# First loads in larger pieces, x by halves of the batch, and a new order of the first and last steps of a conditional GRU

## The chip, the cores and the metric

One core of one Trainium2 chip runs the whole program. The metric is the device time of one execution in microseconds; the kernel before takes 1233.74 us in the median of three runs. Readings of its trace are of one profiled execution.

## The reference, cut to what matters

Batch 64, 128 steps, input and hidden width 512, all fp32:

```
def step(h, inp):
    x_t, prop = inp
    comb = concatenate([x_t, h])
    z = sigmoid(comb @ Wz + bz)
    r = sigmoid(comb @ Wr + br)
    h_cand = tanh(concatenate([x_t, r * h]) @ Wh + bh)
    h_new = (1 - z) * h + z * h_cand
    h_next = where(prop, tanh(h_new @ Wp + bp), h_new)   # prop: every 4th step but the last
    return h_next, h_new
out = x + all h_new
```

Each W of a gate is 1024 x 512: its upper 512 rows meet x_t, the lower 512 meet h. The first h is an input (called cond in the profile, h0 in the code).

## The kernel before, in words

**Layout.** The batch is split into two halves of 32 (h = 0, 1), a width of 512 into four quarters q. A tile such as `xj`, x of one step, has on its 128 partitions the 32 samples of each of the four quarters, and the two halves side by side. VectorE turns it by 32x32 blocks into `xT`, the stationary operand of TensorE. `wx` holds the upper rows of the three gates, as pieces (gate, k) with k = 0 to 3 of 128 rows each; `wh` the lower rows; `wp` Wp.

**The x part** does not depend on the recurrence. For steps 0 to 3 it is plain: 48 units of 16 matmuls, one for each (step, gate, k), into the banks a, x, q, y, b and z (function `plain`); VectorE adds the bias and stores the result in `cp`. From step 4 on, four steps are a group, and their products follow a scheme of seven products in place of eight, on two levels. Its operands are sums: of weights (`tw`, `tf`, `tt`; made once, by `weigh` on GpSimd, called POOL, and VectorE, called DVE) and of xT (`s12r`, `s`, `o` and others, POOL). A batch's results leave the banks q, a, y and x by copies on ScalarE (called ACT) and additions on DVE, are put together in `st` by POOL, and reach `cp` by a DMA for one half and a copy on ScalarE for the other (`place`).

**The h part** of a step: the products hT with wh for r (bank e for half 0, bank r for half 1), sigmoid on ScalarE, r*h and its transpose `rhT` on DVE, the products rhT with Wh, tanh, and the update of h, its transpose `hT`. From the third step to the fifth last the products with r and z share seven products (`sa`, made by POOL from hT).

**Start.** TensorE first runs 42 idle matmuls on zeros. Three one-row loads bring br, bz and bh; `spread` multiplies them with a row of ones, so that all partitions hold them; it is one operation of 12 groups of matmuls, four for each bias, and the units of the x part stand behind it on TensorE. ScalarE copies its result out.

**Order.** A planner holds each operation with its engine, what it reads and what it writes. The order of all operations is the table ORDER, a compressed list of positions; each engine executes its own in that order. Loads are issued by an engine's queue: SP, ScalarE (`actq`) or POOL (`poolq`). The transfers of SP and ScalarE share eight counters, dealt out in turn; POOL's have eight of their own. A transfer waits, at the head of its engine, until the one that used its counter eight transfers ago has landed (`[waits DMAHW5_49]` in an order). So a load on ScalarE can hold ScalarE's later work.

Lines below ORDER move up by some 43 in the changed kernel: the helper of all products is line 412 before and 406 after, the spreading 925 and 882, the transposes of x 566 and 523, the sums of weights 611 and 568, the bias loads 493 and 473, the copy to cp 884 and 841.

Of the kernel before, what the change touches and what calls it, by code (L numbers as in the profile page):

```python
# [172 lines left out]
1ET<%P9Y}BV#L@GFvmexgoPDBU|Fy%+F2SnGsiIu&H!pR%g)ijNG2FC~M6u%V1$?Mq)f}$nehM3|^91lxYPvW$3pTW$^sW;tcxE+|1tWcjsm1W$H7%neUL
<8B~|i>NDH2c;=v-pP2)*8JSs`_qE#0yVEn%0J8w|p?_^gW@=`T%CyWB5U3_2PaeEIwV7%Fnv|)@pvf7zDubj68Gb@WoR}G(k;i4k8JW*X)tQNaaha;j<P
0yMayWyP!DWrjlx4iqj7UdiMrDNZOl5|U(o9K)6=q0zrYJ*7GKCqf2<}P&2$Y{u$v{$+!H<(qqyFS!f*vIOiE=Nwmmv90BHT`p!rw^lCU=q>3D1jAgij8`
H<G@Dzm{A}ZYNigQ2eh;NpB)vOlD>-CYKYR?@NXVD927G*>g$uB+O1GXA=8FayrR7nb^mmv!jX4eiQ9W*#0EFCt-V%aCfpl*_DL5lI|o9yONzrS{K5tNw_
7^ydfKtZOO)DOJXs{-I{Dj_~iQ=6WiXJY)#VNi<c*MM-r`0P<zsrEKg`#(w?+FK?i)>9m!fC`~b8k%`k6++MXb_5&Ee_ZAcmuW^s!W*;tTJyfB%U@M?X+y
-n&8naoVSAR#<0nV#UO$(&?rGBdfDysp$FQxa)vGCBFY^hR~US0xjZ*AFF?2@)nH<C95Xg$kHfCNEEd(wsqKlb6ONV-kK|raYMdE9FT=^5R4&FO@=E3cfT
Mo6r-`)KST(M5VL@T1g@gPlhKlElNfwMTt_FKs-DtNa)7osgeY2aWc490O1Iz193r;52^$%w;0^0gglNPLHH;hmJEZ6@{|6U?M(2)nBI@?$GAVf7vsC}ot
WH?@pODM4sOKU^%#?@@vZn~d^P6q?f6;@!`zJ+--)jSs$gx%h4@ljm)wf8*f<xTi!a2eC+>~U0`v=U`gE-KLV7AT&cr8U{REUV@rf7($6_=ZABj~D9gPpg  # L180
2V-;~9*&)T@xIvI8#~VK_&~fn4gz#A_IAhKz8G6wgIl(_FOE0G|7MySWAq2KCf3))>*CdbwNI+v8ME#2gLr+sDn@JLHStOaSH}Kt*FwD#tIOlcL~W04p8H
ixEaLW<VYMNqzg!$6nOhJqj%7427RCA)33ub!u`JJu5s#+FGveuB`R_3_4b+s_u8F6{bVD*3bWJ=tUY}UgVuU8f9I1}+gcwbUC&Azw6>(Lpjf>wK7mtl6#
$Wq7nh=-874cU~AuoljG)B^>Cw){bjf|xu@rYO|iATrM@OXHPiU&(kEEU3ckstF#@i4gf&lSWau~ZiGLQy=BE`&1%(kMUnAEgJ<tRI5@bbp$TfL%f!r`hB
5y>x!ey5qZPax+bDrHOVUeLZ~>s9j5Qs4q?M<@BenrZ1)O#q`BALejbP`LxuN=Fg@TemFjr7S5(mruoy5*2R5kUdYF1(<jn04_oL+`Wf+P`cQh1htupJ44
88ueI(8HrR^cd(+AS_f%N_~v${dD?dh&`dPkZ?+tTLdbo3h|4A-UCrCAWHPH#xB1|*$nv^q`GE7H8n+SAUmw6`+dmj21|bZgpif7F`x+S8t!w5FTV9qF9g
o^DAmN-s$_r=7)VYjK(`OzTbQMwn8vBt0*!pG>0@>4j+*&rUma=~?MHK&L)EGtD?uo32eGGAlhbJuS^@(lu#>tJ4&rs<cv-u1q80tuyJ0H0IHm^w{*I^qB
O7G<$ta8jVYr0+z+)X*L?ftE18_F)dGzOqZw2()<Wm-jIH?G(9T)>hSdF^oTTHJh)SoeidXv`juh`hYkZjEL{N12NtIJ-RXgdK8^~~P##6B|9^_|AX=YR*
yHG4#2!X>BkBHNO8cXS5q<gr?A(v~qubGwbM8gtW<<&L=tgusVz;6z5!VN&+=%+3YY`!rBh(x9g1H{8OkauyaWTRdA;RY)4);V{Pejf{^mIgfqEpe?=xOJ
CRD%gV8=Z*GMCg2kj8jo{8b0}*i;hPJqTHG2V00wX_ec99v=8*&2px*lgHgOILg}5666}b&Bh}v)1>MosNbxpD@H@U3Z-_QW+oBDCBJ9$&5$BN3Xia3{m6
3}&BFk=%IwNaYq_jnPd(<A8D<VVhh?YlxXo*%uO;KC4EV>gdjas2E1&_48s1eW-HGpr3{HAD0<TpHViz8p71ka1+MPxzb|7swb6D^1^R~O;BNdGyW9?gu5  # L190
8xf*YBQ!PQ(Bw$0jxZLhqA5{T#0z**#6B7qRYnyN8yhk95vCTRqayrmczcyZ#nHF0S`ZaPSStd93I~tj(O17VJ>8!gNEJk18AwTm(SuYzP<oKMpVIpwy_f
1w-Ag?H-UmKRp{>zfi0*<B??6#+r`AOB?UW+lNTKVgJE_~L>nU_E#XnBnfGy#TTd8X)bR%^$brlAz59aI&IPr1{e!umlZl(GF2%S%H=Tlcw=TmU|ICLg;G
KEg16!<`ulF$o>Q-@MWeQJM7-j|Zmfz;mAo|LNWO7Y#PBD^!jKffcTrnjYdWlL&DYJ2Lx%cJg;xIeWuCFY*mmJ&CnkgzGWJ~hY<Fkhb<vNgs2xIVQeg=n%
aMdP(8+L2nF>PW3hErY&1McbjYgQ0DyxD9k`s^tmdrKzQ<SZjilf+ZkT)|gt9a^kQF+W%^Vy=NLzO8|3I^HcPv3sX*GN}iKioSL2D=BDbPN!-j7$>?MntV
~T!2kwDd3w>G&O;1fprMJResez15PNC|Q_<>F<Qxj9-gcRn4iqyCi&yPvbcgs^{DT7i}p5jKqox*RU5h<}C^~HizeoD+wEs2!32SR0S>T|OrB%u2t|2RZ<
!~T$m@n;9ZTOmVtLV7)<FWn5UhBw0NP+z83!keI9x*T2$?}UT(a@YsF0=ycsRjFQx=%uhXq!*#c7Y2{>q0*3|(xvchNY967LfR8v44=LTCxRUu)6?O(koA
VAASdKRcrxUU4<4srb~ro={%CkSBuAhf1{@0sT97&j{a|<?qz6L0FAVpGcuz=}*Bz1}T_LT;+e4>2+!<~QG2RuTZQ-DSzw~y8UE#*CIEA*uD6=ut*F&%++
#YTMudfZ)hG<>5Ce+aCa9!9Lrqq=oS{1GgSAansVMjO$JMCdR_`ym`u-zKAh7MU8TJ2$TXj!dcOK3HO8vbt=HHDTvFVxM&;i3@Lhla5v{NvnkVOST=3VTA
N&j2+eoCy~<Bh+Vyv@To#H((}A$?s}Hc~&?%6iH1u3Hq<$rKk#dPDK@=!i^0TQXW=>QhE6E(h#9hAsiz^c|?e$;bBQQCLA7)4yBKUt`L=k1tHB37o}KXNC
yH2{0MQ@!+^UNe1N#y0m3(fn$(@(o2q^%xF1{#ZUkRP*Mh#_CJ=q~a&S37(k0M+fpjrIy}<?88LStAi@@FhEf3Gb()j?L3-})B^4UN<8=MKG(}CC%oC?kc  # L200
_2K6)1QLHP5Kn@;81NT@o&cQ=jtA^ya4Zmy2IA@9NZ=d@2;q+e<VbKbI2<5!FxV4lyMkT8!GKe{0`wx98Ey-91ls~_YoKj`jZL682WZGhygpbTXaZgn@Ny
y6cz#{b5qxraAf}cDa!1e>i2Xr(kb6p69<&DHvS3-TGH3}<F0UzA8Z-w@!5<p~)&{etpdnz*!9v(r3?|bM*b9OM0h=FKivw04)CWn(>H;%jGXj5lP#46tL
3&#73x7&5H3*E!0drFmK|ZBb2K<D;tqM#wAuuNf(*g_hxWKFq#s?pk2Iavx;FthS2+D$ZbWj=?v^*FQ1Zx9*ILzosxEmva!oVpG3W6e_;|vSlD+rXwKEEK
a`h8y76+G~beqVU!t}ov4d34Ly*bU$0&{hAskNf;S|E7Q2e*^PZ{9YfudC{*5U+wkT>*svwwI2VhFP!l&_yRlUpYnTro?Y}$_~-r8KBAL?W1t^F{q!;aD2
z|}^oalI7moR7{6qdR;1S?q;89;*5FCVv9`FzNbiaSl7x($nK7X$-(%lg4_jmh~f~Tc}KIM=3gLBIE`a9tXj`(|g(&dv~KHctj`(6GPf1A(k^f|)q@HhB$
# [97 lines left out]
def kernel(  # L303
# [145 lines left out]
    def rows(ap, t, h):  # L449
        return ap[ts(h, V), t, :].rearrange("b (q j) -> q b j", q=NQ)  # L450
# [50 lines left out]
    for i in range(3):  # L501
        load_bias(i)
# [817 lines left out]
```

## Time and profile before

| | us |
|---|---|
| runs | 1235.84, 1233.74, 1231.88; median 1233.74 |
| span of the profiled execution | 1229.9 |
| median of the runs less that span | 3.8 |
| TensorE (PE) busy | 1213.1 |
| POOL busy | 942.4 |
| DVE busy | 864.0 |
| ScalarE (ACT) busy | 789.1 |

The span runs from the first instruction to the last. In a row of a timeline stand the start, the length, the engine (PEld is TensorE's weight load, a q behind a name the engine's queue), the line, the operation with out<-in, and in brackets the idle time ahead of it with what ended it. In the stretches each engine has its busy time and its count, then come the granted TensorE clock, the busy share of the DMA engines and GB/s.

### The profile page before, as it was taken

The numbers are of one execution on the slowest core, as the hardware profiler recorded it, in microseconds if no ns is written. First come the engines' busy times: TensorE is split into PE (matmuls) and PEld (weight loads), VectorE is DVE, ScalarE is ACT, GpSimd is POOL, SyncE is SP. The second block draws the span as 40 slices with busy tenths as digits, with TensorE's granted clock in tenths as the row PEclk, the third lists the DMA queues.
The fourth block names the chain that finished last, engine by engine and source line by source line (L and its number), as shares of the span: only waits on it lengthen the run. The fifth ranks groups of instructions, "written<-read, shape, count | busy, mean of one in ns | idle before, by whom it ended". The sixth has DMA issues, their size and how long they took to land.

```text
span 1229.9 us, 85504 instructions
## 1 busy us (share of the span) xinstructions
PE 1213.1 (99%) x37666; PEld 1139.7 (93%) x37666; DVE 864.0 (70%) x2831; ACT 789.1 (64%) x2305; POOL 942.4 (77%) x1489
## 2 busy tenths in 40 slices
PE   8999999999999999999999999999999999999997
PEld 6879999999999999999998999999899999999987
DVE  4677677777767777667776767767676776767774
ACT  0466666676666766666776666676666767666653
POOL 6977777887768787777887777887777878697761
PEclk9999999999999999999999999999999999999999
DMA  7412121221212222121221222212122211222121
GB/s 191 128 46 54 39 62 50 59 61 48 54 49 53 60 59 53 40 61 49 64 60 39 55 54 54 64 42 56 50 56 58 60 42 51 57 55 59 39 58 37
DMA packets 92754, 71.50 MB, mean 58 GB/s; under 512 B 7515, under 2 KB 88283, under 8 KB 92382
## 3 DMA queue, kind: packets, MB, share of 16 engines
q1 hardware_dynamic: 91512, 65.37, 20.4%
q8 instruction: 296, 4.85, 1.7%
q0 software_dynamic: 512, 0.53, 0.2%
q14 instruction: 76, 0.62, 0.2%
q10 hardware_dynamic: 358, 0.14, 0.0%
HBM read 24.84 MB, written 16.78 MB: 34 GB/s over the span
## 4 chain that ended last, share of the span: by engine, by line
PE 95%; DMA 2%; SPq 1%; issue 1%; DVE 1%; ACT 0%; POOL 0%; POOLq 0%; ACTq 0%; DVEq 0%
PE ps_e L412 16%; PE ps_r L412 16%; PE ps_b L412 13%; PE ps_y L412 12%; PE ps_q L412 12%; PE ps_x L412 12%; PE ps_z L412 10%; PE ps_a L412 6%; DMA wx<-in_L_cond_Wr_dram 0%; DMA wx<-in_L_cond_Wh_dram 0%; DMA wx<-in_L_cond_Wz_dram 0%; SPq L483 0%; DMA wh<-in_L_cond_Wr_dram 0%; SPq L538 0%; POOL st L860 0%
## 5 line engine op out<-in xcount | busy, mean ns | idle before, releaser
L1070 POOL TENSOR_TENSOR sa<-hT 128x64 f32<-128x64 f32 x244 | 76.3, 322 | 145.4 <-DVE hT L975 92.0
L412 PE MATMUL ps_z<-wh,sa 128*32 128x128 f32 x3904 | 160.8, 273 | 0.9 <-POOL sa L1070 0.9
L860 POOL TENSOR_TENSOR st<-mb,mb 128x768 f32<-128x768 f32 x77 | 141.1, 1833 | 23.0 <-ACT mb L827 18.6
L884 ACT COPY cp<-st 64x384 f32<-64x384 f32 x248 | 125.9, 509 | 25.0 <-DVE keep L1078 11.5
L412 PE MATMUL ps_e<-wh,rhT 128*32 128x128 f32 x4096 | 141.1, 273 | 0.3 <-issue 0.3
L412 PE MATMUL ps_r<-wh,rhT 128*32 128x128 f32 x4096 | 140.4, 273 | 0.7 <-DVE rhT L975 0.6
L412 PEld LDWEIGHTS ps_z<-wh,sa 128*32 128x32 f32 x3904 | 122.5, 110 | 8.7 <-issue 2.4
L412 PEld LDWEIGHTS ps_r<-wh,rhT 128*32 128x32 f32 x4096 | 121.1, 110 | 4.6 <-DVE rhT L975 1.2
L1164 POOL TENSOR_TENSOR xj<-xj,h 128x256 f32<-128x256 f32 x127 | 93.3, 735 | 40.6 <-DVE h L1147 40.3
L412 PEld LDWEIGHTS ps_e<-wh,rhT 128*32 128x32 f32 x4096 | 120.9, 110 | 2.6 <-issue 0.8
L975 DVE STREAM_TRANSPOSE hT<-h 128x128 f32<-128x128 f32 x318 | 98.0, 310 | 34.5 <-ACT h L1022 21.0
L860 POOL TENSOR_TENSOR mb<-mb,mb 128x768 f32<-128x768 f32 x60 | 110.1, 1834 | 13.0 <-ACT mb L827 12.4
L1018 ACT COPY ps_r<-cp 128x128 f32<-128x128 f32 x256 | 69.1, 270 | 56.2 <-DVE h L1147 26.5
L566 DVE STREAM_TRANSPOSE xT<-xj 128x256 f32<-128x256 f32 x128 | 83.4, 655 | 18.2 <-DMA xj<-in_x_dram 11.6
L412 PE MATMUL ps_y<-tw,s 128*32 128x192 f32 x1456 | 94.3, 326 | 0.3 <-issue 0.3
L1078 DVE TENSOR_TENSOR ps_z<-ps_z,keep 128x128 f32<-128x128 f32 x244 | 71.6, 294 | 27.4 <-PE ps_z L412 21.3
L412 PE MATMUL ps_e<-wh,hT 128*32 128x128 f32 x2144 | 86.7, 273 | 1.9 <-ACT ps_e L1018 1.8
L1078 DVE TENSOR_TENSOR keep<-ps_b,cp 128x128 f32<-128x128 f32 x244 | 67.9, 281 | 28.2 <-PE ps_b L412 27.5
L860 POOL TENSOR_TENSOR st<-mb 128x768 f32<-128x768 f32 x47 | 86.1, 1832 | 1.7 <-ACT mb L827 1.0
L1070 POOL TENSOR_TENSOR sa<-hT,sa 128x64 f32<-128x64 f32 x244 | 78.9, 323 | 9.3
L975 DVE STREAM_TRANSPOSE rhT<-rh 128x128 f32<-128x128 f32 x256 | 78.9, 309 | 6.8
L412 PE MATMUL ps_b<-wh,hT 128*32 128x128 f32 x1952 | 80.3, 273 | 0.0
(183 smaller groups left out, 3561.1 us busy)
## 6 DMA issues: line engine op xcount, KB each, us to landing
cp<-st SPq DMA_DIRECT2D x248, 96.0 KB
out_dram<-xj SPq DMA_DIRECT2D x254, 64.0 KB
xj<-in_x_dram SPq DMA_DIRECT2D x248, 64.0 KB
wx<-in_L_cond_Wz_dram SPq DMA_DIRECT2D x8, 128.0 KB
wx<-in_L_cond_Wh_dram SPq DMA_DIRECT2D x8, 128.0 KB
wh<-in_L_cond_Wr_dram SPq DMA_DIRECT2D x8, 128.0 KB
wh<-in_L_cond_Wz_dram SPq DMA_DIRECT2D x8, 128.0 KB
wh<-in_L_cond_Wh_dram SPq DMA_DIRECT2D x8, 128.0 KB
```

Source lines behind the costliest of these rows:

```text
L412: nc.tensor.matmul(dst, lhsT=lhsT, rhs=rhs, start=start, stop=True, skip_group_check=True)
L566: lambda: nc.vector.transpose(out=xT_(g)[:, i].rearrange("p c (a h b) -> p h (c a) b", a=S, h=S), in_=xj(t).rearrange("p h (e k) -> p h k ...
L860: el("pool", 768, lambda: nc.gpsimd.tensor_add(dst, a, b), reads, writes, rank=FOLD)
L884: el("act", 384, lambda h=h, own=own: nc.scalar.copy(cp_(2 * g + a)[own, nb, h].rearrange("p b g u -> p (b g u)"), st_(n)[own, h].rearrang ...
L975: add("dve", 0.23, lambda: nc.vector.transpose(out=dst, in_=src), reads, writes, land=0.08, main=True)
L1018: el("act", n, lambda: nc.scalar.copy(dst, src), reads, writes, "+" + bank, main=True)
L1070: tensor(lambda: nc.gpsimd.tensor_sub(sa[:, n], a, b), reads, [("sa", t, n)], n=64, engine="pool")
L1078: tensor(lambda: nc.vector.tensor_add(dst, a, b), reads, writes, used_)
L1164: el("pool", 256, lambda: nc.gpsimd.tensor_add(x_out, x_out, h_(new_)), [("h", new_, 0), ("h", new_, 1)] + xk_, xk_)
```

## The change

1. x(0) to x(3) and the first h come by halves of the batch, 64 KB each in the form 128x1x128 (`load_first`): the first half of x(0) on SP, all others on ScalarE's queue. Before, x(0) came as four quarters of 32 KB on SP and ScalarE, x(1), x(2) with x(3), and h as 16 quarter loads on POOL's queue. x(4) to x(7) come by halves too, the even ones on SP and the odd ones on ScalarE; before, in eight loads of all four steps on SP.
2. The upper rows of the gates come as 12 pieces of 256 KB (128x512), where there were two such pieces and 20 of 128 KB (32x2x512). The lower rows and Wp come in four pieces of 256 KB each, where there were eight of 128 KB.
3. ORDER is another table. The sequence of operations of each engine differs in about the first seventh and the last eighth of the program and is the same between. No matmul and no operation of DVE is added or removed; POOL loses its 16 load issues.

```diff
-    def load_step(t, q, engine):
-        load(
-            engine,
-            lambda: queue(engine).dma_start(
-                out=xj(t)[part(q)], in_=x[:, t, ts(q, J)].rearrange("(h b) j -> b h j", h=S)),
-            [("xj", t, h, q) for h in range(S)], size=32.0, cost=0.4,
-        )
+    def load_first(t, engine, hs=(0, 1)):
+        for h in hs:
+            load(engine, lambda h=h: queue(engine).dma_start(out=xj(t)[:, h, :], in_=rows(x, t, h)),
+                 [("xj", t, h, q) for q in range(NQ)], size=64.0, cost=0.6, few=True)
...
-    def load_wx(i, k, wide=False):
+    def load_wx(i, k):
...
+        load("sp", lambda: nc.sync.dma_start(out=wx[:, k, i, :], in_=w[:, k]),
+             [("wx", 0, i, k)], size=256.0, cost=0.43)
...
+    def load_wh(dst, w, keys, over=(), ks=K):
+        if over:
+            add("sp", 0.001, lambda: None, (), [(*keys, "room"), *over])
         for q in range(NQ):
             load(
                 "sp",
...
+                lambda q=q: nc.sync.dma_start(
+                    out=dst[part(q), :ks], in_=w[ts(q, P), :].rearrange("(k e) n -> e k n", e=V)[:, :ks]),
+                [(*keys, k, q) for k in range(ks)], [(*keys, "room")] if over else [], size=64.0 * ks, cost=0.43,
             )
...
-    for q in range(NQ):
-        load_step(0, q, ("sp", "actq")[q % 2])
+    load_first(0, "sp", (0,))
+    load_first(0, "actq", (1,))
     for i in range(3):
         load_bias(i)
+        load_first(i + 1, "actq")
     for i in range(3):
-        for k in range(0, K, 2):
-            if i == R and k == 0:
-                load_wx(i, k, True)
-                load_wx(i, k + 1, True)
-            else:
-                load_wx(i, k)
+        for k in range(K):
+            load_wx(i, k)
...
-    for q in range(NQ):
-        load_step(1, q, "poolq")
     for h in range(S):
...
         load(
-            "poolq",
...
+            "actq",
+            lambda h=h: nc.scalar.dma_start(out=h_(0)[:, h, :], in_=h0[ts(h, V)].rearrange("b (q j) -> q b j", q=NQ)),
+            [("h", 0, h)], size=64.0, cost=0.6, few=True,
         )
...
+    for t in range(Q4, 2 * Q4):
+        load_first(t, "actq" if t % 2 else "sp")
```

What moves, at three places. ScalarE from its first instruction (wt is the tile of the bias rows, xj x, h_98 the first h). Before:

```order
L444 DMA xj<-in_x_dram 32x2x128 x2
L493 DMA wt<-in_L_cond_br_dram 1x512
L511 ACT_TABLE_LOAD
L511 ACTIVATE dummy<-wt 1x1 [waits Pool_49]
L493 DMA wt<-in_L_cond_bz_dram 1x512 [waits DMAHW0_49]
L493 DMA wt<-in_L_cond_bh_dram 1x512 [waits DMAHW1_49]
L930 COPY xj<-ps_y 128x3x2x64 [waits PE_49]
```

After:

```order
L440 DMA xj<-in_x_dram 128x1x128
L473 DMA wt<-in_L_cond_br_dram 1x512
L440 DMA xj<-in_x_dram 128x1x128 x2
L473 DMA wt<-in_L_cond_bz_dram 1x512 [waits DMAHW0_49]
L440 DMA xj<-in_x_dram 128x1x128 [waits DMAHW2_49]
L440 DMA xj<-in_x_dram 128x1x128 [waits DMAHW3_49]
L473 DMA wt<-in_L_cond_bh_dram 1x512 [waits DMAHW5_49]
L488 ACT_TABLE_LOAD
L488 ACTIVATE dummy<-wt 1x1 [waits Pool_49]
L440 DMA xj<-in_x_dram 128x1x128 [waits DMAHW1_49]
L440 DMA xj<-in_x_dram 128x1x128 [waits DMAHW3_49]
L494 DMA h_98<-in_cond_dram 128x1x128 [waits DMAHW4_49]
```

Between br and bh stand now both halves of x(1), and both of x(2), and the counter for which bh waits, 5, belongs to the second piece of Wr; counter 3 to the first piece, and counters 0 and 2 to the first half of x(0) and to br.

DVE around the r*h of the second step (h_99 is the h of that step; rh and rhT are r*h and its transpose). Before:

```order
L854 TENSOR_TENSOR mb_85<-ps_x,c_0_90 128x2x6x32
L851 TENSOR_TENSOR mb_85<-ps_y,q_0_91 128x2x6x32
L566 STREAM_TRANSPOSE xT_81<-xj 128x2x4x32
L1036 TENSOR_TENSOR rh_102<-ps_r,h_99 128x128
L975 STREAM_TRANSPOSE rhT_103<-rh_102 128x128
```

After:

```order
L808 TENSOR_TENSOR mb_85<-ps_y,q_0_91 128x2x6x32
L568 TENSOR_TENSOR tw_70<-wx 128x768
L568 TENSOR_TENSOR tw_69<-tw_70,wx 128x768
L568 TENSOR_TENSOR tw_71<-wx,tw_69 128x768
L993 TENSOR_TENSOR rh_102<-ps_r,h_99 128x128
L932 STREAM_TRANSPOSE rhT_103<-rh_102 128x128
```

Three sums of weights that stood some thirty operations earlier, ahead of the first step's r*h, now stand directly ahead of the second step's.

ScalarE in the last step that uses the seven products, around the copies to cp. Before:

```order
L1022 ACTIVATE ps_e<-ps_e 128x128 [waits DVE_49,PE_49]
L884 COPY cp_84<-st_88 64x384 [waits DVE_49,Pool_49]
L884 COPY cp_83<-st_89 64x384 [waits Pool_49]
L1022 ACTIVATE ps_r<-ps_r 128x128 [waits DVE_49]
L1022 ACTIVATE cand_105<-ps_e 128x128 [waits PE_49]
```

After:

```order
L979 ACTIVATE ps_e<-ps_e 128x128 [waits DVE_49,PE_49]
L1046 COPY cand_105<-ps_r 128x128 [waits PE_49,Activation_49]
L979 ACTIVATE ps_r<-ps_r 128x128 [waits DVE_49]
L784 COPY mb_87<-ps_x 128x2x6x32 [waits PE_49]
L975 COPY ps_r<-bias_p 128x128 [waits DVE_49]
L841 COPY cp_83<-st_88 64x384
L979 ACTIVATE ps_z<-ps_z 128x256 [waits DVE_49]
```

Before, two copies to cp stand between the sigmoids of the two halves of r; now the first of them stands behind the second sigmoid.

315 lines of the change are left out of this document (134 added, 181 removed).

## The prediction

> **What bounds the kernel now.** I read the page's totals first, then the stretches of busy time, then the first and last microseconds row by row. The totals and the chain that ended last:
>
> ```profile
> span 1229.9 us, 85504 instructions
> PE 1213.1 (99%) x37666; PEld 1139.7 (93%) x37666; DVE 864.0 (70%) x2831; ACT 789.1 (64%) x2305; POOL 942.4 (77%) x1489
> PE 95%; DMA 2%; SPq 1%; issue 1%; DVE 1%; ACT 0%; POOL 0%; POOLq 0%; ACTq 0%; DVEq 0%
> ```
>
> TensorE is busy in all but 16.8 us (1229.9 - 1213.1). The change neither adds nor removes a matmul, so everything that it can win or lose lies in these 16.8 us, or is idle time that it adds to them. Where they lie, by stretches (the columns are PE, PEld, DVE, ACT and POOL busy, granted clock, DMA share, GB/s):
>
> ```profile
> 0.00:40.00 40.00, 34.77 (x906) 26.94 (x910) 20.71 (x29) 4.69 (x12) 30.11 (x40) 1.00 0.79 199
> 60.00:80.00 20.00, 17.88 (x506) 14.55 (x498) 13.80 (x33) 11.22 (x31) 18.48 (x28) 1.00 0.12 31
> 200.00:1100.00 900.00, 899.08 (x28040) 852.35 (x28036) 642.34 (x2149) 604.24 (x1764) 706.36 (x1132) 1.00 0.21 54
> 1190.00:1230.00 40.00, 31.51 (x1067) 28.77 (x1056) 22.39 (x79) 15.82 (x54) 9.13 (x12) 0.99 0.15 39
> ```
>
> So 5.2 us are idle in the first 40 us, 2.1 between 60 and 80, 8.5 in the last 40, and only 0.9 in the 900 us of the middle, whose order does not change. Even before detail this caps the gain: to be faster by 3.7 us, the 0.3% that I take as the least a measurement tells from no change, the new version must remove a quarter of that idle time. The first microseconds on TensorE (start, length, what; in brackets the idle time before it and what ended it):
>
> ```profile
> 7.04 0.20 PEld L925 LDWEIGHTS ps_y<-wt 1*32 1x32 f32 x8 [0.41 <-DMA wt<-in_L_cond_bh_dram]
> 9.30 1.08 PE L412 MATMUL ps_x<-wx,xT 128*32 128x128 f32 x16 [1.61 <-DVE xT L566]
> 10.15 1.93 PE L412 MATMUL ps_a<-wx,xT 128*32 128x128 f32 x32
> 15.42 0.62 PE L412 MATMUL ps_x<-wx,xT 128*32 128x128 f32 x16
> 30.13 0.64 PE L412 MATMUL ps_r<-wh,hT 128*32 128x128 f32 x16 [0.24 <-DMA wh<-in_L_cond_Wr_dram]
> ```
>
> The busy time up to 7.7 us is idle work on zeros and the spreading of the three bias rows over partitions, whose last third waits for bh until 7.04. The first product that counts starts at 9.30, held by the transpose of x(1), which came through POOL's queue. From there on each microsecond of delay is a microsecond of the span, as long as nothing else waits.
>
> **The change, the start.** x(0) to x(3) leave POOL's queue, and x(1) is no longer last. In its place stands bh. Before, ScalarE issued it as its fifth transfer; its start and that of bz, and a wide piece of Wr on SP:
>
> ```profile
> 2.82 0.24 ACTq L493 DMA_DIRECT2D wt<-in_L_cond_bz_dram  x1
> 3.11 0.26 ACTq L493 DMA_DIRECT2D wt<-in_L_cond_bh_dram  x1
> 2.11 5.12 DMA wx<-in_L_cond_Wr_dram
> 6.19 4.73 SPq L469 DMA_DIRECT2D wx<-in_L_cond_Wz_dram  x8
> L454 SPq DMA_DIRECT2D xj<-in_x_dram x240: 529/574/853, 45.3 to 1135.6; - x120
> ```
>
> SP's and ScalarE's transfers share eight counters, dealt out in program order, and a transfer waits until the one eight before it has landed. In the new order bh's predecessor on its counter is the second piece of Wr (`[waits DMAHW5_49]` in the order of ScalarE), and two halves of x(2), the second of which waits for the first piece of Wr, stand ahead of it in the same queue. The second piece took 5.12 us from issue at 2.11 to 7.23. In the new program SP has one half of x(0) (0.57 us, the L454 row) and one piece ahead of it instead of two 32 KB loads and one piece, so it starts about 0.35 us earlier, but it now runs beside four half loads of x. I take its landing at 7.0, between 6.5 (earlier by all of that and a little of what the three 128 KB pieces ahead of 6.19 cost it) and 8.3 (held up by the halves). bh itself took 3.93 us before, from 3.11 to 7.04, of which some was queueing. Behind the halves of x(2) I give it 3.5: lower bound 2.9, upper 4.5. So bh lands at about 10.5, in 9.4 to 12.8, and behind it stands the last third of the spreading, some 0.6 us (in 7.04 to the end of that group at 7.7). The first product starts at 11.1 instead of 9.30: **+1.8 us**, from +0.7 to +4.1.
>
> A second way to the same landing goes by rate. When half loads of x run alone, later on:
>
> ```profile
> GB/s 10 5 5 0 0 0 0 0 0 41 36 46 41 0 0 0 0 0 41 56 61 20 41 67 77 82 72 67 241 51 41 61 61 72 61 82 82 87 77 77
> GB/s 0 0 0 0 0 133 106 154 79 193 266 258 263 316 346 334 228 193 223 234 281 228 205 228 234 240 158 217 281 246 182 246 240 240 217 217 275 275 240 211
> ```
>
> The first row (45 to 49 us, slices of 0.1 us) is SP issuing such halves back to back: some 80 GB/s at most, 0.8 us for 64 KB. The second (0 to 14 us, slices of 0.35) has its first bytes at 1.75 to 2.1 us and 200 to 340 GB/s while wide pieces run. Six halves (x(0), x(1), x(2)) at 0.8 us and three pieces of Wr at 256 KB / 260 = 1.0 us, if both compete for the same few lanes, end at 2.0 + 4.8 + 3.0 = 9.8 us, and bh behind them at about 10.5. The two ways agree.
>
> The Trainium skill gives the reason for that rate: a transfer from these queues is cut over the largest number of engines, 16 at most, that divides the slowest dimension of both sides ("DMA: Bandwidth & Descriptors", section "Why a DMA increments its semaphore by 16 and not by 1"). For halves of x in four quarters that would be 4 of 16; the 80 GB/s beside 340 agree. The same page says that loads started from several queues share the same engines and save only the issuing ("Issuing engines are not separate DMA queues"), which speaks against a gain from the second queue; it is rival C below.
>
> The slow first products (16 in some 0.8 us at 9.30 to 11.0, against 0.44 at 15.42) stay slow whenever they start; I move them along and cost them at nothing more.
>
> **The change, the weights and POOL.** Operand sums for the batch products are POOL's, and they begin once the first piece of Wh is in:
>
> ```profile
> 18.21 1.77 POOL L611 TENSOR_TENSOR tf<-wx 128x384 f32<-128x384 f32 x1 [6.59 <-DMA wx<-in_L_cond_Wh_dram]
> 12.88 4.72 DMA wx<-in_L_cond_Wh_dram
> 9.52 2.11 POOL L527 DMA_DIRECT2D h<-in_cond_dram  x4
> 71.99 0.62 PE L412 MATMUL ps_r<-wt,hT 128*32 128x128 f32 x16
> 73.88 0.86 PE L412 MATMUL ps_q<-tt,s12r 128*32 128x192 f32 x16 [1.26 <-ACT ps_a L827]
> 70.66 0.65 PE L412 MATMUL ps_z<-wh,sa 128*32 128x128 f32 x16 [0.85 <-POOL sa L1070]
> 69.87 0.45 POOL L645 TENSOR_TENSOR s<-o 128x128 f32<-128x128 f32 x1
> 70.56 1.82 POOL L860 TENSOR_TENSOR st<-mb,mb 128x768 f32<-128x768 f32 x1
> ```
>
> From 18.21 POOL runs nearly without a pause (18.48 of 20 us busy in 60 to 80), and at 70 TensorE catches up with it: 0.85 us for sa and 1.26 us for a copy at the end of POOL's st, its transfer and ScalarE's copy. That is the 2.1 us. Before, eight pieces of 128 KB were in flight, each some 4.7 us from issue to landing, so 1 MB per 4.7 us. In the new program the pieces are of 256 KB on the same eight counters, and of the eight loads of x(4) to x(7) between wx and wh four go to ScalarE's queue. The first piece of Wh is issued when the first half of x(2) has landed, at about 9.5, and lands at 13.5 to 14, some 4.5 us before 18.21 (2 to 6). POOL also loses its sixteen issues, but it was waiting for Wh then, so they are worth nothing by themselves. With 4.5 us of lead and a TensorE that is 1.8 us later, POOL is 6 us ahead where it was 2.1 us late: **-2.1 us**, bounds 0 and -2.1. The 0.24 us at 30.13 for wh goes too: **-0.2**.
>
> What takes some of it back is the new order. TensorE reaches the first product with tt and s12r five units of 0.44 us sooner, so 2.2 us of the lead are spent there. And of the DVE's long sums (tw, 128x768), which before were done ahead of the first step's r*h, three now stand directly ahead of the second step's r*h and its transpose, for which the products with Wh wait:
>
> ```profile
> L611 DVE TENSOR_TENSOR tw<-wx 128x768 f32<-128x768 f32 x4 | 6.0, 1514 | 1.7 <-DMA wx<-in_L_cond_Wh_dram 1.7
> L611 DVE TENSOR_TENSOR tw<-tw,wx 128x768 f32<-128x768 f32 x2 | 3.4, 1693 | 0.0
> L611 DVE TENSOR_TENSOR tw<-wx,tw 128x768 f32<-128x768 f32 x2 | 2.4, 1218 | 0.0
> 72.41 1.04 DMA cp<-st
> ```
>
> Three of them take 1.5 + 1.7 + 1.2 = 4.4 us (the groups tw<-wx, tw<-tw,wx and tw<-wx,tw). They cost nothing if they begin while r is still being made, since TensorE then has z and batch products of 0.33 and 0.44 us to go on with; if they begin only when r is ready, the last part of them is bare. I give **+0.8 us**, half of one such sum; bounds 0 and 2.5 (one in full, and the 1.0 us of a transfer cp<-st like the one at 72.41 that the sooner products meet).
>
> **The change, the end.** In the last 40 us TensorE waits for the recurrence itself:
>
> ```profile
> 1194.76 1.05 ACT L884 COPY cp<-st 64x384 f32<-64x384 f32 x2 [0.99 <-DVE keep L1078]
> 1196.81 1.08 PE L412 MATMUL ps_r<-wh,rhT 128*32 128x128 f32 x32 [0.62 <-DVE rhT L975]
> 1198.58 1.08 PE L412 MATMUL ps_e<-wp,hT 128*32 128x128 f32 x32 [0.69 <-DVE hT L975]
> 1219.58 1.08 PE L412 MATMUL ps_e<-wh,hT 128*32 128x128 f32 x32 [0.73 <-ACT ps_e L1018]
> ```
>
> Two copies of 0.5 us each stand ahead of the sigmoid of r there; the new order puts them behind it, which frees the 0.62 (and perhaps half of the 0.69). In the last four steps the same matmuls stand between the same waits, with the z products ahead of r; the 0.4 to 0.7 us per step stay, since no other product is left to fill them. At the very end one output transfer now stands ahead of the last tanh on ScalarE and waits for DVE: up to +0.4. Together **-0.5 us**, bounds -1.5 and +0.5.
>
> **The sum.** 1.8 - 2.1 - 0.2 + 0.8 - 0.5 = -0.2 us. Against the profiled execution: span 1229.7. The median of the runs, 1233.74, lies 3.84 us above the span before; with the same outside it, 1233.5.
>
> **Rivals.**
> A, the forecast: later start, no hole at 70, 1233.5 (own range 1231 to 1236.5). Chance 0.50.
> B, the start costs little and the rest comes in full: bh lands at 9.4 (+0.7), hole and wait for wh gone (-2.3), nothing new on DVE, tail -1.5, and 1.0 of the 2 us that TensorE loses to issue gaps in 20 to 35 us: -4.1, 1229.6. For it: the page has that many gaps only while loads run. Against it: every term must be at its end. 0.22.
> C, slower: the halves of x starve. If each packet of a half waits its turn behind packets of wide pieces, six halves and the pieces behind them do not end at 9.8 but each half takes 0.8 + 1.0 us, 10.8 us in all, bh lands at 13.5 and the start is at 14.2: +4.9. Then x(2) and Wh are late as well (Wh waits for the first half of x(2)), POOL gains nothing and the hole stays: 4.9 + 0.8 - 0.5 = +5.2, 1238.9. It decides from a landing of bh after 13 us. For it: bh and four half loads share the counters with wide pieces. Against it: bz and bh before took under 4 us beside wide pieces. 0.15.
> D, the changed order stalls by itself: start as forecast, but the DVE's sums cost 2.5 and, the lead being spent on the sooner batch products, the hole is only halved: 1.8 - 1.1 + 2.5 - 0.5 = +2.7, 1236.4. For it: POOL and DVE are the busiest exactly there. 0.10.
> E, it does not bring weights sooner, since 200 to 280 GB/s is the rate and not the counters: 1.8 + 0.3 - 0.5 = +1.6, 1235.3. Against it: 316 to 346 GB/s in the second row above. 0.03.
>
> **How the numbers follow.** Faster than 1230.0 takes nearly all of B and a little of A: 0.21. Slower than 1237.4 takes C, a third of D and little of A: 0.20. The rest, 0.59, is within. The range must reach into B and C: 1229 to 1239.
>
> **What would show it.** In the changed profile: the last third of the spreading (line 882) waits for bh until 9.4 to 12.8, and the first product (line 406) starts behind it and not behind a transpose; POOL's first sum (line 568) starts at 13 to 16; no idle time of over 0.5 us on TensorE in 65 to 80; idle time in 40 to 65 with DVE rhT or hT as what ended it, if D; 0.6 us less at the last gated step. A first product before 9.3, or a busy time under 1211 or over 1215 us, would be against my reading of it altogether.

## The result, and the profile after

The changed kernel takes 1250.55 us in the median of six runs (1248.41 to 1257.54), the kernel before 1233.72: a ratio of 1.0151, 95% interval 1.0130 to 1.0172, some 17 us slower. The forecast of no difference was wrong, and so was the range.

The totals and the chain of the changed kernel, from its page:

```profile
span 1248.5 us, 85420 instructions
PE 1219.3 (98%) x37666; PEld 1144.7 (92%) x37666; DVE 861.8 (69%) x2831; ACT 785.6 (63%) x2305; POOL 929.9 (74%) x1473
PE 92%; DMA 3%; DVE 2%; issue 1%; ACT 1%; SPq 1%; POOL 0%; ACTq 0%; DVEq 0%; POOLq 0%
```

The span is 18.6 us longer. (In the kernels below 1.7 to 2.3 us lie outside the span, so the profiled execution of before must be the quickest of its three, 1231.88; spans differ by some 1.8 us more than medians do.) TensorE's idle time is 29.2 us instead of 16.8, and its busy time, with the same 37666 matmuls, 6.2 us longer. The same stretches of the changed kernel (columns as in the prediction), and two more, 40 to 60 and 160 to 200:

```profile
0.00:40.00 40.00, 30.17 (x734) 23.65 (x735) 10.36 (x20) 3.09 (x6) 7.93 (x14) 0.87 0.75 191
40.00:60.00 20.00, 17.26 (x525) 16.97 (x528) 11.46 (x26) 7.61 (x23) 11.05 (x17) 1.00 0.27 57
60.00:80.00 20.00, 18.90 (x556) 16.72 (x551) 17.85 (x35) 10.41 (x32) 16.12 (x17) 1.00 0.14 36
160.00:200.00 40.00, 36.58 (x1085) 33.24 (x1081) 25.14 (x85) 24.89 (x73) 32.12 (x53) 0.96 0.23 60
200.00:1100.00 900.00, 897.92 (x27960) 853.16 (x27955) 641.12 (x2142) 602.38 (x1758) 703.81 (x1128) 1.00 0.21 53
1208.50:1248.50 40.00, 31.61 (x1048) 28.35 (x1037) 22.18 (x74) 16.82 (x58) 14.51 (x15) 0.95 0.19 50
```

The first 40 us hold 9.8 us of idle time instead of 5.2, at a mean granted clock of 0.87. The hole at 60 to 80 shrank from 2.1 to 1.1. But 3.4 us are idle in 160 to 200, where before had

```profile
160.00:200.00 40.00, 39.98 (x1272) 36.30 (x1263) 29.83 (x99) 27.68 (x83) 32.55 (x56) 1.00 0.21 56
```

and the granted clock is not full there either. TensorE's first rows with waits, the first product (at 11.91), and all its gaps over 0.5 us between 20 and 60 us:

```profile
8.82 0.63 PE L882 MATMUL ps_y<-wt 1*32 1x128 f32 x8 [2.63 <-DMA wt<-in_L_cond_bz_dram]
11.33 0.65 PE L882 MATMUL ps_y<-wt 1*32 1x128 f32 x8 [1.88 <-DMA wt<-in_L_cond_bh_dram]
11.91 1.08 PE L406 MATMUL ps_a<-wx,xT 128*32 128x128 f32 x16
20.20 1.96 PE L406 MATMUL ps_z<-wx,xT 128*32 128x128 f32 x64 [0.82 <-DVE xT L523]
32.57 1.98 PE L406 MATMUL ps_q<-wx,xT 128*32 128x128 f32 x34 [2.57 <-issue]
40.96 0.74 PE L406 MATMUL ps_q<-wx,xT 128*32 128x128 f32 x18 [1.71 <-issue]
46.44 0.74 PE L406 MATMUL ps_y<-wx,xT 128*32 128x128 f32 x19 [1.78 <-issue]
```

The first product comes behind the third group of the spreading, which waits for bh, at 11.91 instead of 9.30. Three waits of together 6.06 us have no releaser at all: the profile calls them "issue", which means that TensorE stood idle and waited for nothing that it shows. Before had four such gaps, of together 2.08 us; two of them:

```profile
20.26 0.43 PE L412 MATMUL ps_q<-wx,xT 128*32 128x128 f32 x8 [0.51 <-issue]
34.29 0.30 PE L412 MATMUL ps_q<-wx,xT 128*32 128x128 f32 x2 [0.91 <-issue]
```

And in the changed kernel the first row behind the longest gap runs at half speed: 34 matmuls in 1.98 us, where 18 take 0.74 later. The clock of three neighbouring stretches (ahead of it, behind it, and on) says the same:

```profile
29.00:32.50 3.50, 1.00 (x36) 0.73 (x25) 2.11 (x5) 0.00 (x0) 0.00 (x0) 1.00 1.06 220
32.80:36.20 3.40, 3.40 (x73) 3.40 (x68) 1.40 (x3) 0.00 (x0) 0.00 (x0) 0.50 1.06 217
36.30:40.00 3.70, 2.96 (x60) 1.47 (x53) 0.56 (x2) 1.13 (x3) 1.65 (x3) 1.00 1.07 224
```

The waits in 160 to 200 us on TensorE, then DVE's and SP's rows just ahead of the first of them:

```profile
172.26 1.11 PE L406 MATMUL ps_x<-tt,xT 128*32 128x192 f32 x16 [2.42 <-DVE mb L811]
177.76 0.86 PE L406 MATMUL ps_y<-tw,s 128*32 128x192 f32 x16 [0.69 <-POOL sa L1027]
171.14 0.63 DVE L523 STREAM_TRANSPOSE xT<-xj 128x256 f32<-128x256 f32 x1 [2.79 <-DMA xj<-in_x_dram]
171.69 0.52 DVE L811 TENSOR_TENSOR mb<-ps_x,c 128x384 f32<-128x384 f32 x1
154.83 4.79 SPq L1124 DMA_DIRECT2D out_dram<-xj  x2
164.19 0.56 SPq L445 DMA_DIRECT2D xj<-in_x_dram  x1
168.04 0.57 SPq L445 DMA_DIRECT2D xj<-in_x_dram  x1
```

DVE works in order: a transpose of x stands ahead of mb and waits 2.79 us for its load, and TensorE waits for mb. The loads of x stand on SP behind output transfers (line 1124), of which the pair at 154.83 holds the queue for 4.79 us: an output transfer waits for GpSimd's sum x + h, whose next one ends at 159.04, and the loads behind it wait too.

Because the middle of the program is the same in both, I also follow POOL's addition x + h, once per step. At the sixteenth step the changed kernel is 14.75 us late, at the 126th 17.5, at the end 18.6: four fifths are lost by then, 212 us into its span. The same figure for every kernel below, from one profiled execution each. (Two of these executions are not typical of their kernel: that of `before_wh256` is the fastest of four, 1237.78 against a median of 1242.50, and that of `before_warm` the slowest of twelve, 1240.43 against 1235.20.)

```
us later than before at step 16:
changed 14.75       loads_only 7.9        order_only 8.2       before_wh256 4.75
after_wh128 7.8     after_wh128_bias 7.2  after_wh128_sp 11.4  after_wh128_sp2 3.9
loads_wh128_bias 2.25  loads_x1_first 5.7  loads_x_only 11.8   before_wx256 1.7
order_sp2 5.6       before_warm 3.1       before_x1 -0.6       before_x1_warm -0.15
before_x1b 0.9
```

### The profile page after: what moved, and what is told of

The parts are those of the page before. It is cut to its first block, busy times and chain, and to the rows that moved or that the text cites. A ratio compares the mean times of both kernels' runs of the same rounds, so it can differ in the third digit from the quotient of the medians.

```text
span 1248.5 us, 85420 instructions
## 1 busy us (share of the span) xinstructions
PE 1219.3 (98%) x37666; PEld 1144.7 (92%) x37666; DVE 861.8 (69%) x2831; ACT 785.6 (63%) x2305; POOL 929.9 (74%) x1473
## 4 chain that ended last, share of the span: by engine, by line
PE 92%; DMA 3%; DVE 2%; issue 1%; ACT 1%; SPq 1%; POOL 0%; ACTq 0%; DVEq 0%; POOLq 0%
PE ps_r L406 15%; PE ps_e L406 15%; PE ps_b L406 13%; PE ps_y L406 11%; PE ps_q L406 11%; PE ps_x L406 11%; PE ps_z L406 9%; PE ps_a L406 6%; DMA xj<-in_x_dram 1%; DMA out_dram<-xj 1%; DMA h<-in_cond_dram 1%; DMA wx<-in_L_cond_Wz_dram 0%; DMA cp<-st 0%; SPq L1124 0%; SPq L445 0%
```

## The experiments

The theories: **F**, large pieces of the recurrent weights keep the DMA engines so full that TensorE's own instructions come late (the "issue" gaps); **O**, the new order stalls by itself; **S**, the bias rows behind halves of x on ScalarE set the start. Ratios are to the kernel before.

### Loads or order

`loads_only`: the loads of the change, all other operations in the order of before. `order_only`: the reverse.

> The changed kernel's loads (256 KB pieces, x and h by halves on SP and ScalarE) with the order of every other operation as before. Theory L (the loads cost the front): the first product at 11 to 12.5 us in place of 9.3, the idle time on TensorE that the profile calls issue at 5 to 7 us in the first 50 us in place of 2.1, and no waits of over 0.5 us between 100 and 200 us; 1238 to 1244 us. Theory O (the new order alone costs it): 1232 to 1236.

> The loads as before, with the changed kernel's order of every other operation. Theory O: the waits between 140 and 182 us stay (3.8 us in the changed kernel, and a spell at half the granted clock behind them), issue idle stays near 2 us: 1238 to 1245 us. Theory L: the waits between 140 and 182 come from the late start and go; 1232 to 1237.

Measured: 1.0061 (1.0042 to 1.0079) and 1.0066 (1.0041 to 1.0092). Each half costs some 8 us alone; together they make 1.0127 of the 1.0151. So both theories get the time that they forecast, each for its half. In `loads_only` the issue gaps are 3.7 us, fewer than forecast, and bz, bh and x are waited for. In `order_only` the wait for mb (a sum of the batch products on VectorE) is still there, and a spell of half clock behind it:

```profile
165.78 0.86 PE L407 MATMUL ps_x<-tt,xT 128*32 128x192 f32 x16 [2.27 <-DVE mb L849]
```

### The pieces of the recurrent weights

`after_wh128` has `load_wh` of before in the changed kernel; `before_wh256` the reverse:

```
-        for k in range(0, ks, 2):              # eight pieces of 128 KB
-            for q in range(NQ): load("sp", ... dst[part(q), k : k + 2] ...)
+        for q in range(NQ):                    # four pieces of 256 KB
+            load("sp", ... dst[part(q), :ks] ...)
```

> The changed kernel with the lower rows and Wp again in eight pieces of 128 KB instead of four of 256. Theory F (TensorE's instructions come in blocks of 16 KB over the same DMA engines, and with 256 KB pieces on eight counters twice the bytes stand ahead of each block): the three issue gaps of 2.57, 1.71 and 1.78 us at 30 to 46 us shrink to some 0.3 to 0.9 each, 6.1 to about 2 us, and the spell of half clock at 33 to 36 us goes: 4 to 6 us faster than the changed kernel, 1244 to 1247. Rival G (the gaps come from the number of units in the new order or from the two queues, not from the pieces): they stay at 5 to 7 us, 1249 to 1253.

> The kernel before with the lower rows and Wp in four pieces of 256 KB, nothing else. Theory F: the issue gaps between 20 and 50 us grow from 2.1 to 5 to 7 us, and perhaps a spell of half clock follows one of over 2 us: 1236.5 to 1240. Rival G: gaps stay at 2 us, 1232 to 1235.

Measured: 1.0083 (1.0060 to 1.0106), which is 0.7% under the changed kernel, and 1.0085 (1.0058 to 1.0111). The second is more than I forecast (1240 is about 1.0051), and more than its trace shows, whose span is 5.8 us longer than that of before. With small pieces no issue gap is left between 20 and 60 us; with large ones before gets two long ones:

```profile
29.10 0.27 PE L409 MATMUL ps_q<-wx,xT 128*32 128x128 f32 x1 [2.28 <-issue]
37.70 0.27 PE L409 MATMUL ps_q<-wx,xT 128*32 128x128 f32 x1 [3.00 <-issue]
```

The gaps lie 128 matmuls, with their weight loads 256 instructions, apart, and each ends 2.6 to 3.1 us after the start of a 16 KB packet on the queue that the profile calls instruction (q8). Starts of those packets:

```
before        11.18 17.48 21.45 26.05 31.49 35.59 39.66 43.51
changed       15.74 19.71 23.24 29.76 37.91 43.66 47.53
before_wh256  10.22 15.84 20.11 26.42 35.08 39.56 43.37
after_wh128   15.08 18.59 22.46 26.18 30.62 34.20 38.03 42.74
```

128 matmuls at 0.44 us per 16 take 3.5 us. Blocks 3.5 to 4.7 us apart (`after_wh128`) keep up, and before has its longest gap, 0.91 us, behind blocks 5.4 us apart; with pieces of 256 KB they come 5.8 to 8.7 us apart ahead of the gaps, and TensorE runs dry. The DMA view of 20 to 48 us (busy tenths in 40 slices; the instruction queue), of before and then of the changed kernel, shows what goes with it:

```profile
DMA  4473148999507999999579998489881676100013
q8 instruction: 7, 0.11, 2.0%
```

```profile
DMA  2222426989999999999999999999999999542001
q8 instruction: 5, 0.08, 1.5%
```

Eight counters hold eight transfers: 1 MB of small pieces, which run out now and then (the 0, 5 and 4 in before), but 2 MB of large ones, which do not before 43 us. F stands: over all kernels here the issue gaps between 20 and 60 us add up to 3.7 to 6.1 us with pieces of 256 KB of the recurrent weights (three kernels) and to 0 to 2.1 us with pieces of 128 KB. That the block waits on the DMA engines themselves, rather than on something that goes with full ones, is the likeliest reading; the records do not name the engine of a packet. Nor is the price the same everywhere: in the order of before the first loads of the change cost 0.61% (`loads_only`) and, with small pieces and the bias rows moved, still 0.25% (`loads_wh128_bias`, below). And with small pieces in the changed order part of the gain goes into a wait of 2.83 us at 63.31, for a copy on ScalarE that stands behind one of bp, which is not loaded before.

The Trainium skill says that instructions come in 16 KiB blocks of 256 by a DMA queue of the sequencer's own, at a cost "mostly hidden" ("Runtime: NRT & Kernel Launch", section "Instruction fetch mechanics"). The blocks agree with the trace; the cost here was up to 3.00 us a block.

### SP's order

`after_wh128_sp` gives the changed kernel with small pieces SP's order of before throughout; `after_wh128_sp2` for 24 entries only, between the loads of x(19) and x(24); `order_sp2` does that on `order_only`:

```
- out 8.0, out 10.0, x20.0, out 9.1, x21.1, out 9.0, out 8.1, x21.0, out 10.1, out 11.0, out 11.1, x20.1, x22.1, x22.0, x23.0, x23.1
+ out 8.1, out 8.0, x20.1, x20.0, out 9.0, out 9.1, x21.0, x21.1, out 10.0, out 10.1, x22.0, x22.1, out 11.0, out 11.1, x23.0, x23.1
```

(step.half; the eight copies to cp among them are left out.)

> The changed kernel with the recurrent weights in pieces of 128 KB, and on SP's queue alone the order of the kernel before (loads of x, out transfers and copies; TensorE, VectorE, ScalarE and GpSimd keep the changed order). Theory Q (the stall at 165 to 172 us comes from SP: x(16) and x(17) are loaded behind the out transfers of step 7, so VectorE's transposes of them and the recurrence's work behind them are late): the wait for mb (2.8 us) and the half clock after it (1.7 us) go, VectorE's transposes there no longer wait over 2 us for a DMA, and the time is 3 to 5 us under the same kernel without the edit (about 1.0045 to 1.0060 of the kernel before). Rival P (the stall lies in the order of VectorE and TensorE themselves): the wait stays at 2 us or more and the time stays at 1.0075 to 1.0090.

> The changed kernel with recurrent weights in pieces of 128 KB; of SP's queue only the 24 entries between the loads of x(19) and x(24) (out transfers of steps 8 to 11, loads of x(20) to x(23), copies of the sixth and seventh group) stand in the order of the kernel before, all else as changed. Theory Q in its local form (the loads of x(20) to x(23) stand behind out transfers of steps that finish later, and VectorE's transposes of them hold up mb and with it TensorE at 165 us): the wait for mb (2.8 us) falls under 1 us, no half clock after it, 3 to 5 us under the same kernel without the edit (about 1.0045 to 1.0060 of the kernel before). Rival P (the loads come late because GpSimd's additions, in the changed order, finish late, whatever SP's order): the wait stays over 2 us and the time at 1.0075 to 1.0090.

> The loads of the kernel before and the changed order of the rest, with the 24 entries of SP's queue between the loads of x(19) and x(24) in the order of before. If SP's entries cost what they cost with the other loads (2 to 3 us), the wait for mb near 166 us falls from 2.27 to under 1 us and the time is 1.004 to 1.005 of the kernel before, where the same kernel without the edit was at 1.0066. What is left would be the start (x(2) wanted sooner, 3.03 us of waiting at 14.6 in that kernel). Rival (the time at that place is lost anyway, in the waits for sa and the copies behind it): 1.006 and more.

The whole swap was worse, 1.0117 (1.0093 to 1.0141): the wait for mb fell to 0.75, but other transfers came late against the unchanged engines. ScalarE waits 5.52 us for bp, where it waited 2.46 in `after_wh128`, and TensorE 4.90 us at 66.8 behind it, where it waited 2.83; one of 1.93 us is new. The local one gives 1.0063 (1.0049 to 1.0077) against 1.0083, and 1.0048 (1.0029 to 1.0066) against 1.0066. Those intervals overlap, so the time alone does not prove it; the rows do. First `after_wh128`, then the local swap:

```profile
165.28 0.95 PE L407 MATMUL ps_x<-tt,xT 128*32 128x192 f32 x16 [2.80 <-DVE mb L813]
```

```profile
161.99 0.86 PE L406 MATMUL ps_x<-tt,xT 128*32 128x192 f32 x16 [0.73 <-DVE mb L812]
170.55 1.08 PE L406 MATMUL ps_e<-wh,rhT 128*32 128x128 f32 x32 [1.21 <-ACT ps_e L976]
```

With the wait the half clock behind it is gone, and at step 16 the kernels are 3.9 and 2.6 us further on; 1.2 and 0.7 of that they had at step 12 already, before the 24 entries. Q holds in its local form, some 2 to 3 us, with the row at 170.55 (1.21 us) taken off already, and rival P, by which the wait would stay over 2 us, falls. What is left of the order's cost begins in `order_sp2` with

```profile
15.16 3.52 PE L407 MATMUL ps_b<-wx,xT 128*32 128x128 f32 x64 [2.99 <-DVE xT L561]
```

a wait for x(2), and behind it 64 matmuls at half clock in 3.52 us, where 64 take 1.96 in before at 20.47.

### The start

`after_wh128_bias` moves the bias rows ahead on ScalarE; `loads_wh128_bias` is the same with the order of before:

```
     for i in range(3):
         load_bias(i)
-        load_first(i + 1, "actq")
+    for i in range(3):
+        load_first(i + 1, "actq")
```

`loads_x1_first` starts from `loads_wh128_bias` and adds `load_first(1, "sp", (0,)); load_first(1, "actq", (1,))` right behind x(0); `loads_x_only` gives it the pieces of wx of before; `before_wx256` gives before the pieces of wx of the change.

> The changed kernel with the recurrent weights back in pieces of 128 KB and with the three bias rows as the second, third and fourth transfer of ScalarE's queue, ahead of x(1) to x(3). Theory S (the first product waits because bz and bh are issued behind x loads on ScalarE and reach the spread last): the waits of line 882 for bz (2.91) and bh (1.93) go, the first product starts at 8 to 9.5 us instead of 12.3, and the time is 2 to 3 us under the same kernel without the move (0.9915 to 0.998 of it; about 1.0060 of the kernel before). Rival S2 (the loads of x are what is late, the bias rows only hide it): the waits move from the bias rows to the transposes of x(1) to x(3), and the time stays within 1 us (1.0075 to 1.0090 of the kernel before).

> The first loads of the changed kernel (x by halves of the batch on SP's and ScalarE's queues) with two mends: recurrent weights in pieces of 128 KB, bias rows first on ScalarE's queue; everything else in the order of the kernel before. If the losses are what theories F (large pieces delay TensorE's instruction blocks), S and Q say, nothing of them is left here: no issue gap over 1 us between 20 and 60 us, first product at 8 to 9.5 us, no wait over 1 us at 160 to 185 us, and 0.997 to 1.001 of the kernel before. Rival (x by halves costs by itself, by later x(2) and x(3) or by more of ScalarE's time): 1.002 to 1.004.

> The kernel of the run with the first loads of the change, recurrent weights in 128 KB, bias rows first and the order of before, with one edit more: the two halves of x(1) are the second transfer of SP's and of ScalarE's queue, ahead of the weights wx and the bias rows. Theory X (the start is late because x(1) is issued behind four pieces of 256 KB of wx and shares the DMA engines with them until 10.5 us; the bias rows were only the wait that showed): the transpose of x(1) starts near 6 us, the first product that needs it at 7 to 8.5 us instead of 11.3, and the time is 2 to 4 us under that kernel (0.9995 to 1.001 of the kernel before). Rival X2 (DMA engines are full from 5 us on, so what x(1) gains the weights wx or x(2) and x(3) lose): the first product starts early, but waits for wx, x(2) or x(3) of 2 us and more follow before 20 us, and the time stays within 1 us (1.0017 to 1.0033).

> The kernel with the first loads of the change, recurrent weights in 128 KB, bias rows first and the order of before, and with the upper weights wx back in the pieces of before (two of 256 KB, twenty of 128 KB). What is left of the change is x(0) to x(7) and the first h by halves of the batch on SP's and ScalarE's queues. If the late x(1) (11.3 us) is the halves' own doing (they share few DMA engines and GpSimd's queue no longer brings x beside the weights), the transpose of x(1) stays after 10 us and the time at 1.002 to 1.003 of the kernel before. Rival (the 256 KB pieces of wx, more bytes in flight, delay them): x(1) lands at 8 to 9 us, the first product at 9 to 9.5, and the time is 1.000 to 1.001.

> The kernel before with wx in twelve pieces of 256 KB, nothing else. If the halves are what is late: as the kernel before (0.9995 to 1.0010), perhaps a first issue gap of 0.5 to 1 us more before 25 us. Rival (large pieces of wx delay x): x(1) on GpSimd's queue lands after 9.5 us, and the time is 1.0015 to 1.003.

Measured: 1.0070 (1.0051 to 1.0090), 1.0025 (1.0012 to 1.0038), 1.0042 (1.0027 to 1.0057), 1.0096 (1.0080 to 1.0113), 1.0005 (0.9995 to 1.0014). The rows with bias rows first, with x(1) first, and with the halves beside small pieces of wx (three kernels):

```profile
11.74 1.94 PE L406 MATMUL ps_x<-wx,xT 128*32 128x128 f32 x32 [4.83 <-DVE xT L525]
```

```profile
18.66 1.05 PE L409 MATMUL ps_z<-wx,xT 128*32 128x128 f32 x16 [5.15 <-DVE xT L530]
```

```profile
10.97 1.08 PE L409 MATMUL ps_x<-wx,xT 128*32 128x128 f32 x16 [3.47 <-DVE xT L542]
22.40 1.08 PE L409 MATMUL ps_a<-wx,xT 128*32 128x128 f32 x16 [7.24 <-DMA wx<-in_L_cond_Wz_dram]
2.70 5.39 SPq L463 DMA_DIRECT2D wx<-in_L_cond_Wr_dram  x4
11.00 9.69 SPq L463 DMA_DIRECT2D wx<-in_L_cond_Wz_dram  x8
```

S falls as the whole story: with the bias rows first the spread is done by 6.3, and TensorE waits for x(1) until 11.74 instead, whose transpose in the changed kernel itself had started at 9.35. Bias rows and halves trade places in one queue. With x(1) first, too, the first product comes at 8.70, and x(3) is awaited until 18.66. What is late is x by halves as a whole, in two ways that no run here separates. A half is long on its way: those of x(1) in the changed kernel are issued by 3.3 us and their transpose starts at 9.35, some 6.5 us after the second one's issue at 2.8, where the quarters on POOL's queue took 5.1 in the median. And the later halves are issued late, x(3) from 10.06 on, since they wait for one of the eight counters that they now share with the weights. The weights wait in turn. Where those are in small pieces (last two rows), SP stands still from 8.1 to 11.0 and then issues eight pieces of Wz over 9.69 us, and Wz is awaited for 7.24 us. SP's own waits in that kernel up to 22 us name the halves (in all, times, longest), and meanwhile the DMA engines are half idle, 0.51 where before has 1.02 (`loads_x_only`, then before):

```profile
SPq L463 <- DMA xj<-in_x_dram: 4.9, 3, 2.9
SPq L463 <- DMA h<-in_cond_dram: 3.0, 2, 2.3
8.00:11.00 3.00, 0.03 (x4) 0.03 (x5) 0.63 (x1) 0.78 (x3) 0.00 (x0) 1.00 0.51 132
8.00:11.00 3.00, 1.70 (x32) 1.58 (x36) 0.63 (x1) 0.23 (x1) 3.00 (x7) 1.00 1.02 219
```

Before, x(1) to x(3) used POOL's own counters. So the large pieces of wx do no harm in before (1.0005) and are what makes the halves bearable in the change. I had the rival's sign wrong there: I expected smaller pieces to be neutral or to help. `loads_x1_first` too came out above both of its forecasts.

### Can the kernel before be beaten at its start?

`before_warm`: `idle(42)` becomes `idle(54)`, and `idle(10)` follows the spread. `before_x1`: x(1)'s four loads go behind those of x(0) on SP and ScalarE; `before_x1_warm` adds 8 and 6 idle matmuls to that; `before_x1b` puts the bias rows ahead of x(1) instead.

> The kernel before with 12 idle matmuls more ahead of the spread of the bias rows and 10 more behind it, nothing else. Theory W (the granted clock of TensorE is set by how long TensorE stood idle: the wait ahead of the first product keeps the clock at half until 14.3 us, which costs the 5 us of work there some 2.5 us): the clock is full from about 7.5 or 10.9 us on, and the time is 1 to 2.5 us less (0.998 to 0.999). Rival W2 (in that stretch the transposes of x(1) to x(3) on VectorE set the pace): the clock is full but waits for xT take the place, within 0.5 us of before. Rival W3 (the added matmuls end too late): first product 0.3 to 1 us later and the clock still at half, 1.0005 or more.

> The kernel before with x(1)'s four transfers taken from GpSimd's queue and put behind those of x(0) on SP's and ScalarE's queues, nothing else. By theory X (the landing of x(1) sets the start) the first product comes at 7.5 to 8.5 us instead of 9.3, x(2) and x(3) land some 2 us sooner on GpSimd's queue, and the time is 0.5 to 1.5 us less (0.9985 to 0.9995 of the kernel before). Rival X2 (DMA engines full from 5 us on; wx sets the pace up to 20 us): waits for wx of 1 us and more, within 0.5 us of the kernel before or up to 1 us slower.

> The kernel before with x(1) on SP's and ScalarE's queues as in the run beside it, and 8 idle matmuls more ahead of the spread of the bias rows and 6 behind it. If the half clock of the first products costs time once the loads no longer set the pace, 1 to 2.5 us under the run beside it (0.9975 to 0.999 of the kernel before); if the loads set the pace up to 20 us, the same as the run beside it within 0.5 us.

> The kernel before with x(1) on SP's and ScalarE's queues, as in an earlier run, but with the three bias rows ahead of it on ScalarE, so that the spread no longer waits for them. First product at 7.5 to 8.5 us instead of 9.30. If the first product sets the time from there: 0.5 to 1.5 us less (0.9988 to 0.9996). If the weights wx set the pace (the DMA engines being full from 5 us on): a wait for wx of 1 us and more between 11 and 17 us, and no difference over 0.5 us.

Measured: 1.0021 (1.0009 to 1.0033), 0.9999 (0.9989 to 1.0008), 1.0023 (1.0011 to 1.0034), 1.0004 (0.9995 to 1.0013). The warm clock came (full from 6.7 us) and bought waits:

```profile
12.88 0.64 PE L409 MATMUL ps_a<-wx,xT 128*32 128x128 f32 x16 [0.93 <-DMA wx<-in_L_cond_Wz_dram]
15.41 0.64 PE L409 MATMUL ps_z<-wx,xT 128*32 128x128 f32 x16 [1.89 <-DVE xT L563]
```

The product at 15.41 started at 14.96 in before, whose matmuls ran at half speed until about 14.0. In `before_x1b` the bias rows are no longer waited for, yet the first product comes at 9.29, held by x(1) on its new queues too. So before 16 us loads set the pace and not the clock. What an earlier first product would be worth is not shown: no edit of before brought it further forward than 9.12. Why the warm kernels are slower rather than equal is not settled. At step 16 they stand at +3.1 and -0.15, and they lose more behind it. The +3.1 come from one place in that execution, a wait of 2.10 us at 49.93 for a copy on ScalarE with half clock behind it from 51.1 to 54.4. None of the runs beat the kernel before.

## Why the prediction was wrong

**The cost left out.** The term for the weights took 256 KB pieces as a gain only: a sooner Wh, a lead for POOL. That large pieces in flight delay TensorE's instruction blocks is in no term and no rival; the "issue" gaps entered once, in rival B, as something that might shrink. They grew from 2.08 to 6.06 us, with a spell of half clock behind the longest, and undoing the pieces gives 0.7% back in the changed kernel, a little under half of the loss. Without it (1.0083 is about 1244) the time would still be out of the range, by the next two.

**The order, +0.8 (0 to 2.5).** Rival D had the kind right, "the changed order stalls by itself", and priced it at 2.7 us for the whole kernel, from DVE's sums ahead of the second step. The order alone costs 0.66%, 8 us. In 40 to 65 us TensorE waits for no rhT or hT, the sign I had named; it waits at 160 to 180 us, for loads of x behind output transfers on SP. I looked at SP's order for the first loads only. Mending 24 entries leaves 1.0048; of that the trace of `order_sp2` shows 2.99 us of waiting for x(2) at 15.16, wanted sooner by this order than POOL's queue brings it, with half clock behind it, and 0.80, 0.85 and 1.29 us at 163 to 173.

**The start, +1.8 (0.7 to 4.1).** The first product came 2.6 us later, bh landed at 11.3, both inside the bounds, and the rows were those that I had named. But bh was not what sets the time: with it out of the way x(1), x(2) or x(3) come late by as much, and in before moving the bias rows ahead did not bring the first product forward (9.29) and bought nothing (1.0004). Rival C, halves that starve, was right about x and wrong about Wh: POOL's first sum started at 16.25, just outside my 13 to 16. The price of the first loads with bias rows and recurrent weights mended is 0.25%.

**The slow first products, at nothing.** They ran 4.7 us at half speed before (9.30 to about 14.0) and 3.8 after (11.9 to 15.7); two new spells of 3.4 us follow the gaps at 32.57 and 172.26. At half lost per spell that is 5.3 us against 2.4: 2.9 of the 6.2 us of busy time. Another 2.3 are in steps 16 to 126, where two executions differ anyway (last section). I said that a busy time over 1215 would be against my reading altogether, and it was 1219.3.

**The hole at 70, -2.1 and wh, -0.2.** The wait for wh went, and the hole shrank by 1.0, though one of 0.79 opened at 81. **The end, -0.5:** the 0.62 at the last gated step went as said, but smaller ones took its place, and the idle time of the last 40 us is the same, 8.4 us (the stretch at 1208.50).

**The median.** I added 3.84 us outside the span. Some 2 us are outside it; the rest was the profiled execution being quicker than the median.

## What to carry to other kernels

Fewer, larger transfers are not free where an engine streams a long program: look at "issue" gaps, at their spacing in instructions and at whether the DMA line ever falls below 9 while they occur. Transfers that share counters or a queue trade with each other, so a load moved off its own queue costs the weights beside it, even when the row that waits names something else. When an order is changed, read the DMA queue's own order through the whole changed stretch: a load behind an output that finishes late stalls an in-order engine long after the start.

## What the runs showed of the hardware that I had not expected

TensorE's instruction blocks lag visibly: 5.8 to 8.7 us between blocks of 256 instructions ahead of the gaps, while large transfers fill the DMA engines, 3.5 to 4.7 us with smaller ones in `after_wh128`, where no gap is left.

Idle gaps of 2.28 to 2.80 us were followed by 3.4 us of half clock in some places (32.57 and 172.26 in the changed kernel, 29.10 in `before_wh256`, 165.28 in `after_wh128`), while one of 3.00 us, at 37.70 in `before_wh256`, was not. The Trainium skill has the gate fall after an idle window of about 3.4 us, watched in free-running windows ("TensorE: Matmul & The Clock Gate", section "Part 1: The HAM clock gate"). The spells' length agrees; the gaps that set them off here were shorter than that.

From step 16 to step 126 the kernels with the order of before run the same operations in the same order on every engine. Yet one profiled execution took 1016.3 us there at the least (`loads_only`) and 1022.8 at the most (`before_warm`), before itself 1016.4. (The changed kernel took 1019.1, with another order near the end of that stretch.) TensorE is idle for 3.6 and 6.6 us of it in these two, so its waits explain about half of the difference. That scatter is as large as most effects sought here, and what lies behind the rest of it stays open; the comparison at step 16 leaves it out.
